# A two-layer convolution kernel: the deformable layer's hats put off by four slots, and half of the projection's loads issued by ScalarE

## The chip, the core and the metric

The kernel runs on one core of a Trainium2 chip. The core has five engines that work beside each other: TensorE (PE in the profile), VectorE (DVE), ScalarE (ACT), GpSimd (POOL) and SyncE (SP, which here only issues DMAs). The time is the device time of one launch in microseconds (us). Between two versions of this kernel the median of a few runs is compared.

## The reference

The input `x` is 32 images of 96 channels and 56 x 56 pixels in float32. Two layers follow each other.

```python
def layer0(x):                                   # inverted bottleneck, 96 -> 576 -> 96 channels
    h = silu(bn(conv1x1(x, fake_quant(w1))))
    h = silu(bn(depthwise3x3(h, fake_quant(w2))))
    s = silu(mean_over_pixels(h) @ se_w1.T + se_b1)
    s = sigmoid(s @ se_w2.T + se_b2)
    return x + bn(conv1x1(h * s, fake_quant(w3)))

def layer1(x):
    mag = abs(rfft2(x))                          # ca: channel weights from mag
    y = x * ca * sa                              # sa: a map from mean, norm and spectrum of x
    aux = concat([y, coord, resize(mean(abs(rfft2(y))))])
    offset = conv3x3(aux, off_w) + off_b         # 9 taps x (x, y)
    gate = sigmoid(conv1x1(relu(conv3x3(aux, dg1_w))))
    y_base = conv3x3(aux, base_w) + base_b
    sampled = bilinear(y, grid + offset)         # 9 samples for every pixel
    y_def = einsum("bcthw,oct->bohw", sampled, def_w) + def_b
    z = (1 - gate) * y_base + gate * y_def
    return relu(batchnorm_over_the_batch(z) + x)
```

## The kernel before

**The pipeline.** `layers` (L943) is one software pipeline over the images. Its main loop runs over 224 bands, seven to an image, each with eight rows of pixels. For a band it samples the deformable layer's inputs in two halves, and beside that it runs two streams for images ahead: `first`, which is `hidden` (L204: layer 0's expansion and depthwise convolution for the image two ahead), and `second`, which is `attend` (L438: squeeze, projection, residual and spectral attention for the image one ahead).

A band has 17 *slots*: seven in each half, and three at its end. In each slot the generator for the band two ahead, `find(n + 2)`, which is `offsets` (L645), takes one step, in the first 14 of them. Then `pump()` raises the slot's number, lets each stream take the steps that are due by then, and runs the closures in the list `later` whose slot has come:

```python
            later.sort(key=lambda e: e[0])
            while later and later[0][0] <= slot:
                later.pop(0)[1]()
```

The instructions are given out in this order. SyncE keeps it strictly. On the other engines a scheduler may reorder them, except for those wrapped in `keep_in_program_order`.

**The hats.** `offsets` computes a band's offsets (`at`, by TensorE and VectorE), writes them to DRAM (`od`, issued by GpSimd, L659), and reads them back repeated over 112 partitions: `ht`, issued by SyncE at L671 some six slots before its use. The *hats* are the bilinear weights max(0, 1 - |position - block row|): an Abs (L674, kept in program order) and a Relu (L675), both on ScalarE and in place. `hd` is their copy in DRAM, issued by ScalarE (L678). `weights_load` (L682) later reads `hd` back twice, as `wc` (L689) and `wr` (L690), four DMAs on SyncE for a half band; `weights` (L694) multiplies the two on VectorE (L696). `sample_tiles` (L717) then takes the samples with matmuls (L725) against `wc`, ScalarE copies them out to `v` (L729), `pack` (L733) moves some of them to the upper partitions (L736, ScalarE), and `deform` (L739) accumulates the result in PSUM (`pd`) with the matmuls of L744.

In the order given out, a band's Abs and Relu come just before the last `pump()` of its second half, and so stand before and between that half's packs.

**The projection.** `hidden` leaves its result in DRAM (`h2d`) as nine units of 128 partitions: four channel chunks of the image's upper half, one with the last 64 channels of both halves, four of the lower half. `attend` projects it in four quarters, each with seven rows of the upper and seven of the lower half. For each, `project_loads` (L302) loads the rows in two halves, each with a tile and a buffer of its own: half 0 has the upper half's four units (784 KB, `hq0`), half 1 the other five (980 KB, `hq1`). The pools `hq` and `ht` have one buffer for each name, so a load waits until the last reader of the load before is done. `project` (L316) runs half 0's matmuls (L324), then half 1's (L324 and L330). `attend` gives out half 0's load of the next quarter one step after half 0's matmuls of this one:

```python
            outs = project(nc, p, rows)
            next(outs)
            yield
            if q + 1 < NQ:
                first = project_loads(nc, p, h2d, q + 1, 0)
```

The first quarter's half 0 is loaded before `squeeze` (L280), whose small activations on ScalarE (L288, L294) compute the scale `s` for layer 0's last weights.

**Other lines in the text.** L153 and L169/L173 are layer 0's expansion (matmul, then activation into `hp`), L262 the depthwise taps on VectorE, L371/L394/L414 parts of the spectral transform, L606/L626 the joint convolution and its activation into `hid`, L629 and L640 copies of the base convolution, L711/L713 the transposes of the image blocks, L783 the combination of a finished band. After the bands comes `normalise` (L1298) without matmuls.

Of the kernel before, what the change touches and what calls it, by code (L numbers as in the profile page):

```python
# [7 lines left out]
FP = mybir.dt.float32  # L8
I32 = mybir.dt.int32
AF = mybir.ActivationFunctionType  # L10
# [23 lines left out]
EW = ER * W  # L34
NBD = H // RB
BW = NBW
TS = 4
NTX = W // TS
# [4 lines left out]
SB = TS + 2 * REACH  # L43
NS = SB * SB
KP = NTAP * TP
# [256 lines left out]
def project_loads(nc, p, h2d, q, half):  # L302

    u0, u1 = ((0, NCH - 1), (NCH - 1, len(UNITS)))[half]
    hq = p["hq"].tile([128, u1 - u0, EW], FP, name=f"hq{half}")
    nc.sync.dma_start(hq, h2d[u0:u1, :, q * EW : (q + 1) * EW].rearrange("u p n -> p u n"))
    return [(UNITS[u][0], hq[:, u - u0]) for u in range(u0, u1)]


# [128 lines left out]
def attend(tc, p, b, x, h2d, pooled, x1, given=False):  # L438
# [7 lines left out]
    if not given:  # L446
        NQ = HH // ER
        first = project_loads(nc, p, h2d, 0, 0)
        yield from squeeze(nc, p, pooled)
        rows = [first, project_loads(nc, p, h2d, 0, 1)]  # L450
        for _ in range(2):
            yield
        for q in range(NQ):
            at = q, q + NQ
            xrs = [residual_load(nc, p, x, k) for k in at]
# [6 lines that stand above are left out]
            os = next(outs)  # L462
            if q + 1 < NQ:
                rows = [first, project_loads(nc, p, h2d, q + 1, 1)]
            yield
            for k, o, xr in zip(at, os, xrs):
                nc.gpsimd.tensor_tensor(o, o, xr, ALU.add)  # L467
                nc.gpsimd.dma_start(x1[:, k * EW : (k + 1) * EW], o)
            yield
# [150 lines left out]
def joint_conv(nc, p, yp, j, hid):  # L620


    w = p["w"]
    pa = bank(p)
    conv3(nc, pa[:, :BW], w["joint"], yp, CJ, j)
    nc.scalar.activation(hid, pa[:DMID, :BW], AF.Relu, bias=w["dg1b"][:DMID])  # L626
    yb = p["yb"].tile([C, BW], FP, name="yb")
    yield yb, pa[OFF0 : OFF0 + NOFF, :BW]
    nc.scalar.activation(yb[BC:], pa[OFF0 + QC :, :BW], AF.Identity, bias=w["cv"]("base_b")[BC:])  # L629
    pb = bank(p)  # L630
    for k in range(NTAP):
        dy, dx = divmod(k, 3)
        r0 = j * RB + dy + PD - 1
        for i in range(2):
            nc.tensor.matmul(pb[i * BC : (i + 1) * BC, : BW // 2].rearrange("p (h w) -> p h w", h=RB // 2), w["base"][:, k],  # L635
                             yp[:C, r0 + i * RB // 2 : r0 + (i + 1) * RB // 2, dx + PD - 1 : dx + PD - 1 + W],
                             start=(k == 0), stop=(k == NTAP - 1))
    yield
    for i in range(2):
        nc.scalar.activation(yb[:BC, i * BW // 2 : (i + 1) * BW // 2], pb[i * BC : (i + 1) * BC, : BW // 2], AF.Identity,  # L640
                             bias=w["cv"]("base_b")[:BC])
    yield


def offsets(nc, p, yp, j, top, hid, ybs, hds):  # L645

    w = p["w"]
    joint = joint_conv(nc, p, yp, j, hid)  # L650
    yb, pa = next(joint)
    ybs.append(yb)
    at = p["off"].tile([NOFF, NTX, 2, TP], FP, name="at")
    for s in range(2):
        nc.vector.tensor_copy(at[:, :, s].rearrange("o t (r c) -> o t r c", r=TS),  # L655
                              pa[:, s * BW // 2 : (s + 1) * BW // 2].rearrange("o (r t c) -> o t r c", r=TS, t=NTX))
    yield
    od = p["dp"].tile([NTX, 2, NOFF, TP], FP, name="od")
    nc.gpsimd.dma_start(od.rearrange("t s o p -> o (t s) p"), at.rearrange("o t s p -> o (t s) p"))  # L659
    yield  # L660
    next(joint)
    yield
    next(joint)
    yield
    next(joint, None)
    nc.vector.tensor_reduce(top, at.rearrange("o t s p -> o (t s p)"), AX.X, ALU.max, apply_absolute_value=True)
    for _ in range(4):
        yield
    ht = p["ht"].tile([SB * NTX, 4, KP], FP, name="ht")
    src = od.rearrange("t s o p -> t (s o p)").unsqueeze(0).to_broadcast([SB, NTX, 4 * KP])  # L670
    nc.sync.dma_start(ht.rearrange("q n k -> q (n k)"), src)  # L671
    for _ in range(6):
        yield
    p["tc"].keep_in_program_order(nc.scalar.activation(ht, ht, AF.Abs, bias=w["blk"]))  # L674
    nc.scalar.activation(ht, ht, AF.Relu, bias=w["one"], scale=-1.0)  # L675
    yield
    hd = p["dp"].tile([4, SB, NTX, KP], FP, name="hd")
    nc.scalar.dma_start(hd.rearrange("x i t n -> (i t) x n"), ht)  # L678
    hds.append(hd)


def weights_load(nc, p, hd, h):  # L682
# [237 lines left out]
def padded(nc, p, a, images):  # L920

    cp = p["cp"]
    yps = [cp.tile([CJ, HY, WY], FP, name=f"yp{i}") for i in range(images)]
    for t in yps:
        nc.gpsimd.memset(t, 0.0)
        nc.sync.dma_start(t[C : C + 4, PD : PD + H, PD : PD + W], a["coord"])
        nc.sync.dma_start(t[CA:, PD : PD + H, PD : PD + W], a["place"])
    p["x2"], p["n_x2"] = [cp.tile([2 * H, CG, WX], FP, name=f"x2_{i}") for i in range(3)], 0
    for t in p["x2"]:
        nc.gpsimd.memset(t, 0.0)  # L930
    p["s4"] = [cp.tile([H, 3, WP], FP, name=f"s4_{i}") for i in range(2)]
    for t in p["s4"]:
        nc.gpsimd.memset(t, 0.0)
    return yps
# [8 lines left out]
def layers(tc, a, dp, x1d, zd, stats, far):  # L943
# [6 lines left out]
    nc = tc.nc  # L950
    B = x1d.shape[0]
    with ExitStack() as ctx:
        p = {"tc": tc, "dp": ctx.enter_context(tc.tile_pool(name="l1d", bufs=3, space=DRAM))}
# [3 lines left out]
        yp, = padded(nc, p, a, 1)  # L957
        top = p["cp"].tile([NOFF, NBD + 1], FP, name="top")
# [20 lines left out]
        streams, later = [], []  # L979
        slot = 0  # L980
# [96 lines left out]
        bands = [(b, j) for b in range(B) for j in range(NBD)]  # L1077
        hids, gates, ybs, hds, ready = [], [], [], [], []

        def find(n):  # L1080
            if n % 2 == 0:
                hids.append(p["hid"].tile([2 * NS, BW], FP, name="hid"))
            hid = hids[n // 2][n % 2 * NS : n % 2 * NS + DMID]
            return offsets(nc, p, yp, bands[n][1], top[:, n % NBD : n % NBD + 1], hid, ybs, hds)

        for n in range(2):
            for _ in beside(find(n)):
                pass
# [20 lines left out]
        for n, (b, j) in enumerate(bands):  # L1109
            if j == 0:  # L1110
                st = p["st"].tile([C, NBD, 6], FP, name="st")
            if j == turn:
                drain()
                refill(b + 1, 3 * RB)
                flush()
                start(b + 1, slots)
            more = find(n + 2) if n + 2 < len(bands) else iter(())
            next(more, None)
            for h in range(2):
# [385 lines left out]
```

## Time and profile before

| | us |
|---|---|
| runs | 9247.16, 9256.04, 9267.85 |
| median | 9256.04 |
| profiled execution, its time | 9239.07 |
| its span in the trace | 9237.3 |
| TensorE, VectorE, ScalarE, GpSimd busy | 8221.8, 7198.1, 5369.4, 2529.9 |
| TensorE waits for `hq` (L324), 31 times | 155.8 |
| TensorE waits for the packs (L744), 73 times | 201.6 |
| ScalarE waits for `ht` (L674), 98 times | 270.2 |

The mean granted clock of TensorE in the profiled execution is 0.933 of full speed. An image takes some 273 us in the middle of the run.

How the lines of the profile are read: a line of a timeline has the start, the length, the engine, the source line, the operation, its output and input, and the number of instructions that were put together; in square brackets stand the idle time of the engine before it and what ended that. In the list of waits each line has the engine and the instruction that waited, what released it, and the total, the number and the longest of such waits. SPq and ACTq are the sequencers of SyncE and ScalarE, as they issue DMAs. Line numbers are those of the kernel before.

### The profile page before, as it was taken

The numbers are of one execution on the slowest core, as the hardware profiler recorded it, in microseconds if no ns is written. First come the engines' busy times: TensorE is split into PE (matmuls) and PEld (weight loads), VectorE is DVE, ScalarE is ACT, GpSimd is POOL, SyncE is SP. The second block draws the span as 40 slices with busy tenths as digits, with TensorE's granted clock in tenths as the row PEclk, the third lists the DMA queues.
The fourth block names the chain that finished last, engine by engine and source line by source line (L and its number), as shares of the span: only waits on it lengthen the run. The fifth ranks groups of instructions, "written<-read, shape, count | busy, mean of one in ns | idle before, by whom it ended". The sixth has DMA issues, their size and how long they took to land. (4 is left out here: it accounts for less than half of the span.)

```text
span 9237.3 us, 138081 instructions
## 1 busy us (share of the span) xinstructions
PE 8221.8 (89%) x52406; PEld 5208.4 (56%) x52406; DVE 7198.1 (78%) x6693; ACT 5369.4 (58%) x10486; POOL 2529.9 (27%) x2611
## 2 busy tenths in 40 slices
PE   5889999999999999899999999999999999999870
PEld 3455565565555556555555655555565655655550
DVE  7587788888888888887888888788888888887333
ACT  2355566666666566665566665566666655666553
POOL 0123233323223322332332223233222323322210
PEclk9889999999999999999999999999999999999985
DMA  2345555555555555555555555555555555554559
GB/s 88 95 137 156 165 166 159 165 150 150 161 163 163 163 164 149 150 157 165 163 157 160 148 153 157 164 167 159 159 152 153 160 166 163 160 160 140 131 181 417
DMA packets 1068764, 1486.54 MB, mean 161 GB/s; under 512 B 590190, under 2 KB 839838, under 8 KB 1055806
## 3 DMA queue, kind: packets, MB, share of 16 engines
q1 hardware_dynamic: 858995, 985.20, 39.2%
q10 hardware_dynamic: 153803, 329.80, 9.8%
q0 software_dynamic: 55296, 162.60, 6.8%
q8 instruction: 421, 6.90, 0.3%
q14 instruction: 249, 2.04, 0.1%
HBM read 1064.29 MB, written 412.65 MB: 160 GB/s over the span
## 5 line engine op out<-in xcount | busy, mean ns | idle before, releaser
L262 DVE SCALAR_TENSOR_TENSOR acch<-hp,w,acch 128x1512 f32<-128x1512 f32 (+1 forms) x2250 | 4397.3, 1954 | 38.2
L606 PE MATMUL mm<-yp,c_jointW 104*128 104x448 f32 x4032 | 1674.2, 567 | 27.7 <-ACT sq L414 19.2
L744 PE MATMUL pd<-v,c_def 128*96 128x224 f32 (+1 forms) x6272 | 1450.9, 378 | 225.2 <-ACT v L736 201.6
L707 POOL COPY ybl<-yp 96x448 f32<-96x448 f32 x896 | 1079.8, 1232 | 1698.5 <-PE mm L711 1697.5
L744 PEld LDWEIGHTS pd<-v,c_def 128*96 128x96 f32 (+1 forms) x6272 | 1046.2, 174 | 524.7 <-ACT v L736 229.2
L606 PEld LDWEIGHTS mm<-yp,c_jointW 104*128 104x128 f32 x4032 | 772.4, 196 | 808.1 <-issue 737.9
L725 PE MATMUL mm<-wc,yt 64*96 64x144 f32 x12544 | 1065.7, 298 | 56.8 <-ACT hp L173 38.0
L169 PE MATMUL mm<-xt,w 96*128 96x392 f32 (+3 forms) x2688 | 1061.2, 529 | 36.4 <-DMA xt<-in_x 33.0
L173 ACT ACTIVATE hp<-mm,sh,inv 128x392 f32<-128x392 f32 (+2 forms) x1216 | 813.2, 673 | 445.4 <-PE mm L169 400.6
L696 DVE TENSOR_TENSOR wc<-wc,wr 128x1008 f32<-128x1008 f32 x448 | 579.5, 1293 | 622.2 <-DMA wr<-hd 614.4
L729 ACT COPY v<-mm 96x288 f32<-96x288 f32 (+1 forms) x2688 | 1001.7, 443 | 100.3 <-PE mm L725 61.3
L725 PEld LDWEIGHTS mm<-wc,yt 64*96 64x96 f32 x12544 | 830.6, 162 | 358.5 <-issue 171.3
L324 PE MATMUL mm<-hq,w3s 128*96 128x392 f32 x2048 | 798.4, 537 | 157.2 <-DMA hq<-h2d 155.8
L635 PE MATMUL mm<-yp,c_base0W 96*64 96x224 f32 x8064 | 828.0, 357 | 0.0
L736 ACT COPY v<-v 32x448 f32<-32x448 f32 x1344 | 755.2, 562 | 29.9
L659 POOL DMA_DIRECT2D od<-at x224 | 186.0, 830 | 1947.6 <-DVE at L655 1386.0
L635 PEld LDWEIGHTS mm<-yp,c_base0W 96*64 96x64 f32 x8064 | 553.2, 135 | 276.2 <-issue 69.3
L713 ACT COPY yt<-mm 128x384 f32<-128x384 f32 (+1 forms) x896 | 350.1, 440 | 519.2 <-PE mm L711 514.5
L324 PEld LDWEIGHTS mm<-hq,w3s 128*96 128x96 f32 x2048 | 340.7, 175 | 513.6 <-issue 323.7
L222 ACT ACTIVATE acch<-acch,sh,inv 128x1568 f32<-128x1568 f32 x288 | 488.6, 1696 | 207.3 <-DVE acch L262 205.0
L626 ACT ACTIVATE hid<-mm,c_dg1b 50x448 f32<-50x448 f32 x224 | 140.7, 628 | 794.7 <-PE mm L606 784.6
L467 POOL TENSOR_TENSOR o<-o,xc 96x392 f32<-96x392 f32 x256 | 366.3, 1431 | 679.3 <-ACT o L334 677.8
(194 smaller groups left out, 9038.8 us busy)
## 6 DMA issues: line engine op xcount, KB each, us to landing
h2d<-acch ACTq DMA_DIRECT2D x288, 784.0 KB
wc<-hd SPq DMA_DIRECT2D x896, 252.0 KB
wr<-hd SPq DMA_DIRECT2D x896, 252.0 KB
hq<-h2d SPq DMA_DIRECT2D x128, 980.0 KB
hq<-h2d SPq DMA_DIRECT2D x128, 784.0 KB
x<-x1d SPq DMA_DIRECT2D x768, 98.0 KB
ht<-od SPq DMA_DIRECT2D x224, 252.0 KB
hd<-ht ACTq DMA_DIRECT2D x224, 252.0 KB
```

What stands on the lines that cost most here:

```text
L169: nc.tensor.matmul(pt[p0 : p0 + w1.shape[1], : rows * W], w1, xts[hf][:, r0 * W : (r0 + rows) * W], start=True, stop=True)
L173: nc.scalar.activation(h1[lo:hi, row0 : row0 + rows, 1 : 1 + W], pt[lo:hi, : rows * W].rearrange("p (h w) -> p h w", h=rows), AF.Silu, bia ...
L262: nc.vector.scalar_tensor_tensor(acc[:, lo:hi], win, wk, acc[:, lo:hi], ALU.mult, ALU.add)
L324: nc.tensor.matmul(pts[half][:C, :EW], w3s[:, ch], hq, start=(i == 0), stop=False)
L606: nc.tensor.matmul(view, weights[:, k], yp[:channels, r0 : r0 + RB, dx + PD - 1 : dx + PD - 1 + W], start=(k == 0), stop=(k == NTAP - 1))
L635: nc.tensor.matmul(pb[i * BC : (i + 1) * BC, : BW // 2].rearrange("p (h w) -> p h w", h=RB // 2), w["base"][:, k], yp[:C, r0 + i * RB // 2 ...
L696: p["tc"].keep_in_program_order(nc.vector.tensor_tensor(wc, wc, wr, ALU.mult))
L707: nc.gpsimd.tensor_copy(yb[:, :, s], blocks)
L725: nc.tensor.matmul(pt[k][:C, (t - lo) * KP : (t - lo + 1) * KP], yt[ps, t], s[ps, t * KP : (t + 1) * KP], start=True, stop=True)
L729: nc.scalar.copy(v[:C, :, lo:hi, k].rearrange("c k t p -> c t k p"), pt[k][:C, : (hi - lo) * KP].rearrange("c (t k p) -> c t k p", t=hi - ...
L736: nc.scalar.copy(v[C:, 1 + 2 * i : 3 + 2 * i], v[i * QC : (i + 1) * QC, KA:])
L744: nc.tensor.matmul(out.rearrange("c q (t x) -> c t q x", x=TS), p["w"]["def"][ks, k], v[ks, k].rearrange("c t s (r x) -> c t (s r) x", r=T ...
```

## The change

The three last steps of `offsets` (Abs, Relu, the write of `hd`) become a function that is put into `later`, four slots further on. The step in which it is put there lies before the band's 14th `pump()`, so it runs in the band's 17th. `hds.append(hd)`, from which the weight loads take `hd`, moves with it. And half 0's loads are issued by ScalarE in program order, while half 1's stay with SyncE.

```diff
@@ project_loads
     hq = p["hq"].tile([128, u1 - u0, EW], FP, name=f"hq{half}")
-    nc.sync.dma_start(hq, h2d[u0:u1, :, q * EW : (q + 1) * EW].rearrange("u p n -> p u n"))
+    src = h2d[u0:u1, :, q * EW : (q + 1) * EW].rearrange("u p n -> p u n")
+    if half:
+        nc.sync.dma_start(hq, src)
+    else:
+        p["tc"].keep_in_program_order(nc.scalar.dma_start(hq, src))
     return [(UNITS[u][0], hq[:, u - u0]) for u in range(u0, u1)]
@@ offsets
-def offsets(nc, p, yp, j, top, hid, ybs, hds):
+def offsets(nc, p, yp, j, top, hid, ybs, hds, defer):
...
     for _ in range(6):
         yield
-    p["tc"].keep_in_program_order(nc.scalar.activation(ht, ht, AF.Abs, bias=w["blk"]))
-    nc.scalar.activation(ht, ht, AF.Relu, bias=w["one"], scale=-1.0)
-    yield
-    hd = p["dp"].tile([4, SB, NTX, KP], FP, name="hd")
-    nc.scalar.dma_start(hd.rearrange("x i t n -> (i t) x n"), ht)
-    hds.append(hd)
+
+    def hats():
+        p["tc"].keep_in_program_order(nc.scalar.activation(ht, ht, AF.Abs, bias=w["blk"]))
+        nc.scalar.activation(ht, ht, AF.Relu, bias=w["one"], scale=-1.0)
+        hd = p["dp"].tile([4, SB, NTX, KP], FP, name="hd")
+        nc.scalar.dma_start(hd.rearrange("x i t n -> (i t) x n"), ht)
+        hds.append(hd)
+
+    defer(hats)
@@ layers, find
-            return offsets(nc, p, yp, bands[n][1], top[:, n % NBD : n % NBD + 1], hid, ybs, hds)
+            return offsets(nc, p, yp, bands[n][1], top[:, n % NBD : n % NBD + 1], hid, ybs, hds,
+                           lambda hats: later.append((slot + 4, hats)))
```

## The prediction

> **What bounds the kernel now.** I read the page's busy line first, then the waits, then the timeline of one image (number 13, 3990 to 4268 us), then a table of windows over it.
>
> ```profile
> PE 8221.8 (89%) x52406; PEld 5208.4 (56%) x52406; DVE 7198.1 (78%) x6693; ACT 5369.4 (58%) x10486; POOL 2529.9 (27%) x2611
> ```
>
> TensorE is the busiest, but 89% holds matmuls at half clock, and VectorE is not far behind. Which of them binds must be read by stage. The waits:
>
> ```profile
> ACT hid L626 <- PE mm L606: 784.6, 173, 13.7
> DVE wc L696 <- DMA wr<-hd: 614.4, 133, 19.1
> ACT ht L674 <- DMA ht<-od: 270.2, 98, 7.4
> PE pd L744 <- ACT v L736: 201.6, 73, 8.0
> PE mm L324 <- DMA hq<-h2d: 155.8, 31, 9.9
> ```
>
> TensorE's own large waits are the last two, and the change touches both: L324 is the projection's first half waiting for its rows (31 times, once in each image but one), L744 the deformable matmul waiting for ScalarE's packs. The third says why the packs may be late: ScalarE stands at the hats' Abs until `ht` has landed.
>
> **Stall A**, SyncE's queue and then TensorE:
>
> ```profile
> 3977.93 0.60 SPq L689 DMA_DIRECT2D wc<-hd  x1
> ...
> 3980.59 0.66 SPq L671 DMA_DIRECT2D ht<-od  x1
> 3983.55 9.08 SPq L306 DMA_DIRECT2D hq<-h2d  x2
> ```
> ```profile
> 3992.13 0.93 PE L169 MATMUL mm<-xt,w 96*128 96x392 f32 x2
> 3997.49 2.25 PE L324 MATMUL mm<-hq,w3s 128*96 128x392 f32 x3 [4.44 <-DMA hq<-h2d]
> ```
>
> The last quarter's first-half load is issued at 3983.55, when its buffer comes free, behind four weight loads and `ht` in the same queue. It lands about 13.9 us later, and TensorE idles 4.44 us.
>
> **Stall B**, ScalarE and then TensorE:
>
> ```profile
> 4034.25 0.55 ACT L394 COPY s<-mm 128x464 f32<-128x464 f32 x1
> 4039.20 0.78 ACT L674 ACTIVATE ht<-ht,c_blk 112x576 f32<-112x576 f32 x1 [4.40 <-DMA ht<-od]
> ...
> 4040.35 0.76 ACT L675 ACTIVATE ht<-ht,one 112x576 f32<-112x576 f32 x1
> ...
> 4041.14 0.33 ACTq L678 DMA_DIRECT2D hd<-ht  x1
> ...
> 4042.13 1.15 ACT L736 COPY v<-v 32x448 f32<-32x448 f32 x2
> ```
> ```profile
> 4042.74 3.30 PE L744 MATMUL pd<-v,c_def 128*96 128x224 f32 x8 [5.04 <-ACT v L736]
> ```
>
> ScalarE waits 4.40 us for `ht`; the packs stand behind the hats, and TensorE behind the packs. Of the 73 such waits some 31 are large like this one.
>
> The windows (columns: length, busy PE, PEld, DVE, ACT, POOL, granted clock, DMA share, GB/s) show what surrounds them:
>
> ```profile
> 3990.00:4004.00 14.00, 9.56 (x22) 4.07 (x21) 8.40 (x5) 4.55 (x8) 5.29 (x7) 0.76 0.85 264
> ...
> 4038.00:4080.00 42.00, 37.10 (x291) 24.66 (x292) 36.55 (x37) 28.51 (x54) 7.60 (x6) 0.92 0.54 147
> 4080.00:4168.00 88.00, 85.04 (x606) 54.32 (x605) 86.70 (x80) 59.26 (x122) 30.08 (x25) 1.00 0.48 129
> ```
>
> After each stall the granted clock falls to one half for about 6.8 us (3996.5 to 4003.3 after A: 0.65 us a matmul for 0.33), and the window's mean is 0.76 and 0.92. In the long stretch from 4080 VectorE is busy 86.70 of 88 us: there it binds, and TensorE's gains are paid out only as far as VectorE comes early to it.
>
> **The change, part by part.** *Hats.* Nothing is added: 224 times an Abs (0.78), a Relu (0.76) and an issue (0.33) move from before the 14th of a band's 17 slots to the 17th. In the built order they leave the place between the second half's packs and stand just before the next band's L626. ScalarE idles there already (784.6/173 = 4.5 us a wait), so 1.9 us of hats are hidden; where a band has no such wait they cost at most those 1.9 us on an engine that is 58% busy. `ht`'s wait goes too, since the load has 9 us more. `hd` is written up to 9 us later; its readers, the weight loads on SyncE's queue, come 7 to 25 us after it now, and the multiply L696 far behind, so I take 0 there. If that cover is gone, a wait like L696's 614.4/133 = 4.6 us appears. On TensorE stall B returns 5.0 idle + about 2.5 of half clock = 7.5 us an image. What is late next is VectorE.
>
> *The load.* 128 issues (0.37 us each) leave SyncE for ScalarE, where each waits for the buffer and holds what follows; the second half's loads stay. On SyncE the half-0 loads no longer hold weight loads and x loads behind them, which I put at 0 (below nothing is possible). By quarter:
> - Last quarter: the issue can't come before 3983.55, but no longer queues behind the weights. Alone, the 784 KB take 3 us of packets; beside the weight loads I take 9.4 us in all, landing at 3993 where TensorE wants them at 3993.06. ScalarE stands 1.5 us at the issue. Of 4.4 to 5.0 us of stall (155.8/31) and 2.9 of half clock, I leave 0.7 for a late landing and return 6.6 to 7.2.
> - Second and third: free at the same time or 2.4 us later, with matmuls further away: 0.
> - First quarter: this load used to be issued some 20 us early (3918.8). ScalarE, in its order, reaches it after L288 at about 3939:
>
> ```profile
> 3938.83 0.25 ACT L288 ACTIVATE s<-acc,seb 24x1 f32<-24x1 f32 x1
> ```
> ```profile
> 3946.48 2.87 PE L324 MATMUL mm<-hq,w3s 128*96 128x392 f32 x8
> ```
>
> The margin is 7.6 to 8.4 us in every image, with four weight loads and `ht` on the other queue until 1.2 us after the need. A new wait of 0 to 4 us; I take 2.5, near the middle, since the packet records show another ScalarE transfer (`h2d`) stretched from 1.8 us alone to 7.3 us beside weights, and `hd` packets alternating one for one with them.
>
> A rule speaks against this part. The Trainium skill, "DMA: Bandwidth & Descriptors", section "Issuing engines are not separate DMA queues", says that transfers from all issuing engines end up on the same 16 DMA engines and that issuing from several saves only sequencer time; by it A would stay, and the sum would be B's part on VectorE alone, 2.3 × 31 = 71 us. The rows above say that A's load is behind others in one queue while packets of two queues alternate, so I go by the rows.
>
> *Sum.* TensorE: idle 155.8 + 201.6, half clock 31 × (2.9 + 2.5) = 167: 524 us in all; less 31 × (2.5 + 0.7) = 99, 425 us. VectorE must follow. Between 3990 and 4076 it idles 20 us, of which 2.93 and 4.68 wait for weight loads (stay), and 3.24, 0.43, 2.51 and 2.32 for things that TensorE's lateness delays: 8.5 us can go, 11.3 with the ping-pong against L414. So the gain is 8.5 − 2.5 (the new first-quarter wait) = 6.0 us an image, × 31 = 186 us. The profiled execution took 9239.07 us (span 9237.3), 17 us under the median of the three runs: 9239 − 186 + 17 = 9070. With 11.3 and a new wait of 0 it is 350 us (8906), with 8.5 − 4 it is 140 (9116).
>
> **Rivals.**
> - *VectorE does not cap.* It has 78%, and the order around 4080 may shift so that all of TensorE's 425 us are paid: 8831. Against it: 86.70 of 88.
> - *Mostly eaten.* The first-quarter wait lets the clock drop (2.5 to 4 + 2.9), so that 8.5 is nearly gone: 8.5 − 6.9 = 1.6 × 31 = 50, or with 8.5 − 5.4 = 3.1, 96: 9160 to 9206; with more of the same, 9225, and if the load only trades A for that wait, no change.
> - *Slower: ScalarE's load crawls.* If 3 us become 12 beside the weight loads, as `h2d` stretched fourfold, and about 2 us pass before the first packet, the first quarter waits 14 − 8 = 6.1 us and 2.9 of half clock, 9.0 in all; the last quarter's load lands at 3997.7, so A stays, and only B's part on VectorE (2.3) is gained: 6.7 × 31 = 208 slower, 9464. It decides from about a threefold stretch: the first quarter then loses 3.1 + 2.9 us and A keeps 1.6 of its idle and the clock, which leaves nothing of the 8.5. For it: `h2d`. Against: that transfer's packets are 6 KB and beside 4 KB ones, and the weight loads end shortly after the need.
> - *It doesn't do what it says.* Excluded for the hats by the built order; for the load only the landing time can tell.
>
> **How the numbers follow.** Main case 0.52 (8906 to 9116), TensorE's full gain 0.16, mostly eaten 0.18 (0.06 of it within 0.2%), slower 0.14. A difference of 0.2%, 19 us, is about what this measurement tells from no change. Faster 0.52 + 0.16 + 0.12 = 0.80, same 0.06, slower 0.14. The range runs from the full gain (8832) to the eaten case's end (9225), leaving out the slower case and the very edge.
>
> **What would show it.** B right: L744 ← L736 falls from 201.6 to under 60, and L674 no longer waits for `ht`. A right: L324's wait for `hq` moves from the last to the first quarter and is about half. VectorE's cap right: its busy share rises from 78% to 80% and it stays above 95% after 4080. Wrong if L324's wait grows above 155.8, if the clock's mean doesn't rise over 0.933, or if L696 ← `wr` grows by more than 100 us, which would mean that `hd` or the weight loads became the late ones.

## The result and the profile after

The changed kernel is slower: 9326.14 us against 9251.6 us (medians of four runs each), a ratio of 1.0083 with a 95% interval of 1.0062 to 1.0104, some 75 us; the time lies above the predicted range, which ended at 9225. Its profiled execution took 9348.17 us, the longest of its four, with a span of 9346.4 us. Lines below the first diff have moved: L324 is now L328, L674 L680, L696 L703, L736 L743, L744 L751, and L306 has become L308 (SyncE, half 1) and L310 (ScalarE, half 0).

The page's busy line and the waits that answer to those of before:

```profile
PE 8363.4 (89%) x52406; PEld 5260.0 (56%) x52406; DVE 7172.3 (77%) x6693; ACT 5379.0 (58%) x10486; POOL 2592.9 (28%) x2611
```
```profile
DVE wc L703 <- DMA wr<-hd: 712.8, 133, 18.4
ACT hid L630 <- PE mm L610: 660.3, 161, 12.6
...
PE mm L328 <- DMA hq<-h2d: 201.0, 64, 8.8
...
PEld mm L391 <- DVE sq L377: 91.9, 31, 6.3
...
PE pd L751 <- ACT v L736: 16.1, 35, 0.9
```

Stall B is off the list: the deformable matmul's wait for the packs, 201.6 us before, is gone, and the 16.1 us that remain wait for a copy. But TensorE's wait for the projection's rows has grown from 155.8 us in 31 waits to 201.0 in 64: two in an image in place of one. And a wait that was not on the list before has come, the spectral matmul L391 for VectorE's reductions, 31 times.

The new wait for `hq`, in the first quarter of image 14: ScalarE's issue, then TensorE.

```profile
4258.63 0.38 ACTq L310 DMA_DIRECT2D hq<-h2d  x1
```
```profile
4266.59 1.22 PE L732 MATMUL mm<-wc,yt 64*96 64x144 f32 x16
4272.13 1.57 PE L328 MATMUL mm<-hq,w3s 128*96 128x392 f32 x2 [4.32 <-DMA hq<-h2d]
```

13.5 us from the issue to the first matmul. The last quarter's load on the same queue, behind SyncE's weight loads and `ht`:

```profile
4305.23 0.59 SPq L696 DMA_DIRECT2D wc<-hd  x1
...
4307.84 0.66 SPq L675 DMA_DIRECT2D ht<-od  x1
```
```profile
4310.11 0.37 ACTq L310 DMA_DIRECT2D hq<-h2d  x1
```
```profile
4319.34 0.93 PE L169 MATMUL mm<-xt,w 96*128 96x392 f32 x2
4325.74 1.59 PE L328 MATMUL mm<-hq,w3s 128*96 128x392 f32 x2 [5.48 <-DMA hq<-h2d]
```

No weight load stands in front of it in its queue any more, and yet 15.6 us pass before its first matmul. Where stall B was, VectorE now stands at the weights' multiply, and TensorE behind VectorE:

```profile
4367.29 1.21 DVE L703 TENSOR_TENSOR wc<-wc,wr 128x1008 f32<-128x1008 f32 x1 [7.63 <-DMA wr<-hd]
...
4369.36 1.15 DVE L377 TENSOR_REDUCE sq<-mm 112x56 f32<-112x448 f32 x2
```
```profile
4370.03 1.15 PE L391 MATMUL mm<-c_FU,x 112*128 112x116 f32 x8 [2.90 <-DVE sq L377]
```

L391 needs a PSUM bank that L377's reductions set free, and these stand in VectorE's order behind the multiply. Over 28 images, 15 of these waits end with L377 as here, and 12 with the landing of `x`, the transform's own input, which SyncE loads. The windows over image 14 (columns as before: length, busy PE, PEld, DVE, ACT, POOL, granted clock, DMA share, GB/s) show the first quarter, the last quarter, the place of stall B, and the long stretch:

```profile
4266.00:4282.00 16.00, 11.69 (x50) 5.99 (x49) 12.09 (x8) 5.94 (x13) 1.33 (x3) 0.89 0.33 107
4318.00:4332.00 14.00, 8.52 (x18) 3.58 (x17) 6.98 (x5) 2.31 (x4) 4.21 (x6) 0.76 0.80 268
4366.00:4408.00 42.00, 37.94 (x288) 23.44 (x287) 38.31 (x38) 27.16 (x53) 9.29 (x6) 0.92 0.58 148
4408.00:4496.00 88.00, 86.14 (x601) 54.93 (x602) 83.85 (x78) 55.59 (x114) 26.96 (x23) 0.96 0.47 129
```

Both places keep a clock of 0.76 and 0.92, and the first quarter, at full clock before, has 0.89.

**One image, stage by stage.** TensorE gives out its work in almost the same order in all these kernels, so the time between two of its own instructions can be compared. The table gives mean us over 28 images, worked out from the traces between starts of L324/L328 and L744/L751; in brackets TensorE's idle time and the time at half clock. "Last" runs from the third quarter's second half to the last quarter's second half and holds stall A; "next" is the band and a half after it; "B" holds stall B.

```
                 first          quarters 2-3  last           next           B              rest           image
before            7.9 (0.0,0.0)  38.2         23.0 (5.0,6.6) 22.2 (0.0,0.0) 41.3 (6.2,7.9) 136.9          269.5
changed          14.9 (3.6,5.0)  38.8         19.8 (2.7,2.9) 22.3 (0.1,0.0) 40.3 (3.6,6.9) 136.0          272.1
hats_only         8.0 (0.0,0.1)  38.2         23.0 (4.9,6.5) 22.2 (0.0,0.0) 40.2 (3.6,6.7) 136.9          268.4
loads_only       13.7 (3.1,3.9)  38.8         19.9 (2.7,3.2) 22.3 (0.1,0.0) 41.2 (6.2,7.8) 136.4          272.3
first_on_sync     8.0 (0.0,0.0)  38.8         20.4 (2.6,4.8) 22.3 (0.0,0.0) 40.2 (3.8,6.3) 136.7          266.4
hats_mul3         9.8 (0.0,1.8)  38.2         23.2 (5.2,6.7) 28.7 (3.0,7.1) 38.5 (3.7,3.1) 137.6          275.9
wide_packets     10.5 (1.1,0.7)  38.8         16.1 (0.3,0.1) 25.7 (1.9,3.3) 39.9 (3.5,6.7) 135.9          266.8
hats_wide         8.0 (0.0,0.1)  38.2         22.8 (4.9,6.5) 22.2 (0.0,0.0) 40.4 (3.8,6.7) 136.5          268.1
first_sync_mul1   8.1 (0.0,0.3)  38.8         19.7 (2.5,3.2) 22.5 (0.2,0.2) 40.5 (3.8,7.0) 140.6          270.3
first_sync_again  8.0 (0.0,0.1)  38.8         20.2 (2.6,4.1) 22.2 (0.0,0.0) 40.3 (3.5,7.1) 136.3          265.8
sync_wide_again   8.0 (0.0,0.1)  38.8         16.2 (0.4,0.1) 26.2 (2.0,4.0) 39.5 (3.5,5.7) 136.4          265.0
```

In the table the changed kernel loses 6.9 us an image at the first quarter and 0.7 before the third quarter's second half. It gains 3.2 in "last", 1.0 at stall B and 0.9 in the rest. The sum, 2.6 us more an image, times 31 is 80 us, close to the 75 us of the medians.

A part of these differences is work that changed its place. Counted by instruction, two of the third quarter's matmuls (L334, 0.65 us) stand in "quarters 2-3" and not in "last" wherever ScalarE issues the loads of quarters two to four. Where it issues the first quarter's too, the ten small matmuls of L291 (1.2 us) stand in "first" and not in the rest, in every second image. Without this moved work the first quarter loses 6.3 us an image, the stretch before the third quarter's second half loses nothing, stall A gives back 2.6, and the rest 0.3.

### The profile page after: what moved, and what is told of

Read it like the earlier page. It is cut to its first block, busy times and chain, and to the rows that moved or that the text cites. A ratio compares the mean times of both kernels' runs of the same rounds, so it can differ in the third digit from the quotient of the medians.

```text
span 9346.4 us, 137984 instructions
## 1 busy us (share of the span) xinstructions
PE 8363.4 (89%) x52406; PEld 5260.0 (56%) x52406; DVE 7172.3 (77%) x6693; ACT 5379.0 (58%) x10486; POOL 2592.9 (28%) x2611
## 5 line engine op out<-in xcount | busy, mean ns | idle before, releaser
L610 PE MATMUL mm<-yp,c_jointW 104*128 104x448 f32 x4032 | 1714.0, 578 | 4.2 <-ACT yt L720 1.9
L714 POOL COPY ybl<-yp 96x448 f32<-96x448 f32 x896 | 1107.5, 1263 | 1802.8 <-PE mm L718 1802.4
L751 PE MATMUL pd<-v,c_def 128*96 128x224 f32 (+1 forms) x6272 | 1417.5, 373 | 19.6 <-ACT v L736 16.1
L610 PEld LDWEIGHTS mm<-yp,c_jointW 104*128 104x128 f32 x4032 | 792.1, 200 | 804.5 <-issue 766.8
L751 PEld LDWEIGHTS pd<-v,c_def 128*96 128x96 f32 (+1 forms) x6272 | 1036.9, 172 | 305.6 <-issue 79.8
L732 PE MATMUL mm<-wc,yt 64*96 64x144 f32 x12544 | 1108.9, 301 | 106.1 <-ACT hp L173 47.4
L703 DVE TENSOR_TENSOR wc<-wc,wr 128x1008 f32<-128x1008 f32 x448 | 577.1, 1288 | 775.3 <-DMA wr<-hd 712.8
L169 PE MATMUL mm<-xt,w 96*128 96x392 f32 (+3 forms) x2688 | 1072.5, 538 | 38.4 <-DMA xt<-in_x 33.4
L732 PEld LDWEIGHTS mm<-wc,yt 64*96 64x96 f32 x12544 | 856.7, 163 | 434.4 <-issue 191.3
L736 ACT COPY v<-mm 96x288 f32<-96x288 f32 (+1 forms) x2688 | 1006.9, 442 | 114.1 <-PE mm L732 76.7
L328 PE MATMUL mm<-hq,w3s 128*96 128x392 f32 x2048 | 834.6, 557 | 208.1 <-DMA hq<-h2d 201.0
L743 ACT COPY v<-v 32x448 f32<-32x448 f32 x1344 | 755.2, 562 | 29.8
L328 PEld LDWEIGHTS mm<-hq,w3s 128*96 128x96 f32 x2048 | 352.5, 181 | 596.8 <-issue 526.2
L471 POOL TENSOR_TENSOR o<-o,xc 96x392 f32<-96x392 f32 x256 | 387.5, 1514 | 856.7 <-ACT o L338 849.5
L720 ACT COPY yt<-mm 128x384 f32<-128x384 f32 (+1 forms) x896 | 350.1, 440 | 444.0 <-PE mm L718 443.1
```

Of the source, the lines that this page charges most:

```text
L169: nc.tensor.matmul(pt[p0 : p0 + w1.shape[1], : rows * W], w1, xts[hf][:, r0 * W : (r0 + rows) * W], start=True, stop=True)
L328: nc.tensor.matmul(pts[half][:C, :EW], w3s[:, ch], hq, start=(i == 0), stop=False)
L610: nc.tensor.matmul(view, weights[:, k], yp[:channels, r0 : r0 + RB, dx + PD - 1 : dx + PD - 1 + W], start=(k == 0), stop=(k == NTAP - 1))
L703: p["tc"].keep_in_program_order(nc.vector.tensor_tensor(wc, wc, wr, ALU.mult))
L714: nc.gpsimd.tensor_copy(yb[:, :, s], blocks)
L732: nc.tensor.matmul(pt[k][:C, (t - lo) * KP : (t - lo + 1) * KP], yt[ps, t], s[ps, t * KP : (t + 1) * KP], start=True, stop=True)
```

## The experiments

### The two halves of the change by themselves

Hats put off, all loads by SyncE (`project_loads` as in the kernel before):

```diff
-    if half:
-        nc.sync.dma_start(hq, src)
-    else:
-        p["tc"].keep_in_program_order(nc.scalar.dma_start(hq, src))
+    nc.sync.dma_start(hq, src)
```

> Only the hats are put off; all projection loads stay on SyncE. Theory (the load is what costs, the hats are worth little): of the changed kernel's stages only the one around the old stall B gains, 1.0 to 2.0 us an image, so 31 to 62 us faster than before (ratio 0.993 to 0.997); L744 <- packs under 30 us, L324 <- hq about 156 as before, no wait at the first quarter. Rival (the late hd is what costs: the weights come later to VectorE): as slow as the changed kernel or slower, ratio 1.005 or more, and VectorE's wait for wr at 700 us or more.

And the loads alone, with `offsets` as before:

```diff
-    nc.sync.dma_start(hq, src)
+    if half:
+        nc.sync.dma_start(hq, src)
+    else:
+        p["tc"].keep_in_program_order(nc.scalar.dma_start(hq, src))
```

> Only half 0's loads go to ScalarE; the hats stay where they were. Theory: the first quarter loses 6.9 us an image, the last quarter gains 3.2, the third loses 0.65, so +4.3 us x 31 = 134 us slower than before (ratio about 1.0145); L744 <- packs stays near 200. Rival (the hats are the slow part): faster than before by 100 us.

Measured: hats alone 9202.45 us against 9256.67 before, ratio 0.9939 (0.9927 to 0.9951), 54 us faster; loads alone 9341.93 us, ratio 1.0104 (1.009 to 1.0117), 85 us slower. The waits of the hats alone, then of the loads alone:

```profile
DVE wc L699 <- DMA wr<-hd: 506.8, 127, 18.2
...
PE mm L324 <- DMA hq<-h2d: 152.1, 31, 7.6
...
PEld mm L387 <- DVE sq L373: 87.9, 31, 4.6
...
PE pd L747 <- ACT v L732: 17.5, 35, 1.2
```
```profile
PE pd L748 <- ACT v L740: 205.8, 75, 8.9
...
PE mm L328 <- DMA hq<-h2d: 178.9, 62, 7.2
```

So the load is what costs, and the hats are a gain. With the hats alone VectorE's wait for `wr` falls (614.4 to 506.8): the later `hd` delays no weights, and the 712.8 of the changed kernel came with the loads, which alone bring it to 741.7. What the loads alone cost was less than expected (85, not 134 us): by the table they lose 5.8 us an image at the first quarter, not 6.9. The two parts do not add up to the whole, 85 − 54 = 31 against 75: in the table 1.1 us of that difference an image is the first quarter's. There the load's last packet comes 12.3 us after its issue with the hats put off and 11.8 without, and more weight packets pass beside it (218 for 161); why is not shown.

### The first quarter's load back on SyncE

```diff
-    if half:
+    if half or q == 0:
         nc.sync.dma_start(hq, src)
```

> Hats put off, the loads of quarters two to four on ScalarE, the first quarter's back on SyncE. Theory: the first quarter's 6.9 us an image go and the rest stays: 2.6 - 6.9 = -4.3 us x 31 = 134 us faster than before (ratio 0.9855). Rival (ScalarE's queue does nothing for the last quarter; its stall was only shorter because TensorE came to it later): like the hats alone, 31 to 62 us faster, L324 <- hq back at about 156.

9155.96 us, ratio 0.989 (0.9878 to 0.9903): 101 us faster than before and 170 us faster than the change. The first quarter is back at 8.0 us, without any wait:

```profile
DVE wc L703 <- DMA wr<-hd: 445.1, 123, 17.2
...
PE mm L328 <- DMA hq<-h2d: 84.3, 32, 8.0
```

One load in four, issued on ScalarE 0.6 to 0.7 us ahead of L288 in every image, where SyncE had issued it some 20 us earlier, makes the difference between 0.8% slower and 1.1% faster. The rival here is refuted: the other three loads on ScalarE's queue do shorten stall A (155.8 to 84.3 us), but leave 2.6 us of idle and most of the half clock.

### Why ScalarE's loads are late: the width of the packets

The trace's packet records of the changed kernel show one and the same transfer, 784 KB in 512 packets of 1568 bytes on ScalarE's queue, under two conditions (means over 28 images, us from the issue):

```
                 first packet   last packet
quarter 2            1.1            3.9        little beside it
quarter 1            1.4           12.3        four weight loads (256 packets of 4032 bytes) and ht
quarter 4            2.9           12.1        the same, and the half-1 load ahead
```

While the weights run, some 47 of its packets pass in a microsecond (512 in 10.9 us), beside some 20 to 35 of theirs; alone 183 pass (512 in 2.8 us). If the engines take turns packet by packet, wider packets must help it. So `h2d` was laid out by quarters: the same bytes and queues, but a load of half 0 has 128 packets of 6272 bytes (and the writes have 1568 in place of 6272).

```diff
-        nc.scalar.dma_start(h2d[u], flat)
+        nc.scalar.dma_start(h2d[:, :, u].rearrange("q p n -> p q n"), flat.rearrange("p (q n) -> p q n", n=EW))
...
-    src = h2d[u0:u1, :, q * EW : (q + 1) * EW].rearrange("u p n -> p u n")
+    src = h2d[q, :, u0:u1]
...
-            h2d = p["dp"].tile([len(UNITS), 128, HB], FP, name="h2d")
+            h2d = p["dp"].tile([HH // ER, 128, len(UNITS), EW], FP, name="h2d")
```

> The changed kernel with h2d laid out by quarters, so that a projection load's packets are 6272 bytes (half 0) and 7840 bytes (half 1) in place of 1568, four and five times fewer of them; its writes become 1568 bytes. Bytes and queues stay. Theory (ScalarE's queue and SyncE's take turns packet by packet, so a load of 512 small packets beside weight packets of 4032 bytes gets a small share): the last packet of the first quarter's load comes 6 to 8 us after its issue in place of 12.3, of the last quarter's 7 to 9 in place of 12.1; both waits of L324's successor go, and the kernel is 5 to 9 us an image, 155 to 280 us, faster than the changed kernel (9050 to 9170 us, ratio to before 0.978 to 0.991). Rival (the 16 engines share out bytes, whatever the packets): last packets still over 11 us after the issue, and the time of the changed kernel, 9326 within 30 us.

9158.39 us, ratio 0.99 (0.9883 to 0.9917), 168 us faster than the change, with only the layout of `h2d` altered (half 1's packets and the writes with it). The last packet of the first quarter's load comes at 9.1 us in place of 12.3, of the last quarter's at 9.2 in place of 12.1; quarter 2, which has no company, hardly moves (3.9 to 3.7). The rival, a share of the bytes whatever the packets, is out. In the first quarter, while only weight packets run beside it, the narrow load passes 48 packets a microsecond beside 26 of theirs, 0.41 of the bytes; the wide one passes 17 beside 24, 0.53 of the bytes, and both together move more (204 GB/s for 181). So width raises a load's share, but the turns are not one for one, and the theory's 6 to 8 and 7 to 9 us were both too short. TensorE's idle at the first quarter falls from 3.6 to 1.1 us, at stall A from 2.7 to 0.3:

```profile
PE mm L328 <- DMA hq<-h2d: 45.6, 37, 3.3
```

A control on whether wide packets are simply faster: the same layout with all loads on SyncE, where weights and loads share one queue.

> Hats put off, all loads on SyncE, h2d laid out by quarters (wide packets). A control on what wide packets do by themselves. Theory (they help only where two queues take turns): in SyncE's one queue the last quarter's load still stands behind the weight loads, its stall stays within 1 us of the 4.9 us idle of the hats alone, and the time is that of the hats alone, 9202 within 30 us. Rival (wide packets are simply faster): the stall is gone or under 2 us, as with ScalarE's queue and wide packets, and the time is near 9131.

9214.32 us, ratio 0.9968 (0.9957 to 0.9979), within 30 us of the hats alone (0.3% above them by the ratios, whose intervals do not meet). Stall A stays whole, 4.9 us idle an image:

```profile
PE mm L324 <- DMA hq<-h2d: 150.5, 31, 7.8
```

So to take stall A away needs both, a queue of its own and wide packets.

### What holds the place of stall B

With the hats out of the way, TensorE's idle at B fell only from 6.2 to 3.6 us. The trace says that VectorE stands at the multiply; so the multiply was given out three slots later:

```diff
-                        ready.extend(weights(nc, p, *ws) for ws in loads[:1])
+                        for ws in loads[:1]:
+                            later.append((slot + 3, lambda ws=ws: ready.append(weights(nc, p, *ws))))
```

> Hats put off, all loads on SyncE, and VectorE's multiply of the weights (wc <- wc, wr) given out three slots later. Theory (what took stall B's place is VectorE standing at that multiply until wr lands, with the reductions behind it that free TensorE's PSUM banks): VectorE's wait for wr falls from about 700 us to under 400, the spectral matmul's wait for VectorE's sq goes, and the kernel gains 3 to 6 us an image beyond the hats alone, 120 to 240 us faster than before (ratio 0.974 to 0.987). Rival (the buffers of wr come free later and SyncE's weight loads with them): no faster than the hats alone, with a new wait of TensorE for wc at the sampling matmuls.

9473.03 us, ratio 1.024 (1.0223 to 1.0257): much slower. Half of the theory is borne out: VectorE's wait falls (506.8 us with the hats alone, 212.9 here), the spectral matmul's wait for `sq` is gone from the upper lines (1.9 us in all), and B shrinks by 1.7 us more, to 38.5. But TensorE's idle at B does not shrink (3.7 us, now mostly at matmuls that wait for ScalarE's L414); what fell is the time at half clock.

```profile
PE mm L728 <- issue: 224.8, 79, 10.2
...
DVE wc L699 <- DMA wr<-hd: 212.9, 74, 17.0
```

The rival was right about the time: TensorE now waits at the sampling matmuls L728 (224.8 us, which the profile puts down to nothing that it shows). The trace tells for what: in 77 of these waits, 223.9 us in all, the matmul starts 0.1 us after VectorE's multiply ends. But in 76 of the 77 the multiply had not waited for `wr`; it came straight behind other work of VectorE. So it is not a late landing of the weights, as the rival had it, that makes these waits, but a multiply that stands too late in VectorE's order. One slot, on the kernel with the first load on SyncE, was tried too:

> As the kernel with the first quarter's load back on SyncE, and VectorE's multiply of the weights given out one slot later (three slots made the hats-only kernel 270 us slower). Theory (the weights land late for TensorE too, so the wait only changes its engine): no faster, 0 to 70 us slower than that kernel, 9156 to 9226 us, the sampling matmuls waiting more. Rival (one slot is free for TensorE and takes VectorE's standing away from the reductions): 1 to 1.5 us an image, 30 to 45 us faster, 9110 to 9125 us.

9268.52 us, ratio 1.0025 (1.0013 to 1.0037), 113 us slower than without it, beyond both expectations. Here L391's wait for `sq` stays as it was (87.6 us), and the loss lies in the rest, 3.9 us an image. There L169 now waits for ScalarE's copy into `yt` (L720), 73.6 us in all where it was 3.5; why is not shown. The two runs say that moving this multiply is not free, and that with it moved L391's wait goes while the idle time at B stays. What bounds this place is left open.

### A version that beats both

Hats put off, the first quarter's load on SyncE, and wide packets:

> As the kernel with the first quarter's load back on SyncE, but with h2d laid out by quarters. Theory (packet turns): only the last quarter's stall is left to win, 2.6 us idle and about 2 us of half clock, of which VectorE lets 2 to 4 us an image through: 60 to 125 us faster than that kernel, 9030 to 9095 us (ratio to before 0.976 to 0.983). Rival (bytes): 9156 within 30 us, the wait for hq still 2.6 us an image.

9131.46 us, ratio 0.9882 (0.9863 to 0.9901). The interval meets that of the narrow packets, so the two were run again side by side:

> The kernel with the first quarter's load back on SyncE again, beside the next one on the same chip: 0.989 of before, within 0.002.

> The same with wide packets again, beside the run above. Theory: the 1.1 us an image that its trace showed less than the one above, x 31 = 35 us, are real: 20 to 50 us faster than that one. Rival: no difference beyond 15 us, since what the last quarter gains is given back at the pd bank two bands later.

Narrow 9136.76 us, ratio 0.9878 (0.9863 to 0.9893); wide 9118.96 us, ratio 0.9862 (0.9847 to 0.9877). Wide is ahead by 18 us in the medians, 0.7 us × 31 = 22 in the traces, between the theory's 20 and the rival's 15, and the intervals meet; that it is faster than before by some 129 us, 1.4%, is clear. The expected 2 to 4 us an image did not come, and the table says where they went. Stall A is gone with all its half clock: "last" takes 16.2 us, 6.9 less than before, of which 0.65 is the moved work and 6.2 to 6.3 the stall. "Next" takes 3.9 more than before, with 2.0 us of idle time that was not there, mostly for VectorE's combination of a band (L790, 1.65 us). The row among the waits, and one such wait in image 14:

```profile
PE pd L751 <- DVE z L790: 48.3, 23, 3.2
```
```profile
4251.29 1.06 PE L751 MATMUL pd<-v,c_def 96*96 96x224 f32 x2 [2.58 <-DVE z L790]
```

TensorE is early at the single `pd` bank, VectorE has not yet combined the band before, and 4.0 us at half clock follow.

## Why the prediction was wrong, point by point

- **The step that failed** is the landing time of a load on ScalarE's queue beside the weight loads. I took 9.4 us for the last quarter and a wait of 2.5 us for the first. Both loads have their last packet 12 us after the issue, and the first matmul comes after 12.9 and 13.1. So the first quarter waits 3.6 us, and as this lies inside the bound of 0 to 4, what undid this term was also the other half of that stall: 5.0 us at half clock, which I had priced only in the rivals. Idle time and the half of 5.0 us make 6.1 of the 6.3 us an image lost there, where the sum had 2.5. The issue itself came where I had put it. Term by term, in us an image: the sum had 6.2 from A, 2.3 from B and -2.5 at the first quarter; the runs show 2.6, 1.0 and -6.3, and 0.3 in the rest.
- **Stall A** was to return 6.6 to 7.2 us; it returned 2.6, since of 5.0 us of idle 2.7 stayed. That ScalarE's queue frees it from standing behind the weights was right, and with wide packets it returned 6.2 to 6.3, near what I had asked of it. What I missed is that a queue of one's own buys only a share of the DMA engines: with 1568-byte packets beside 4032 that was 0.41 of the bytes.
- **The slower rival** had the mechanism: a fourfold stretch, 14 us to land, a first-quarter wait of 6.1 with 2.9 of half clock. I gave it 0.14 because `h2d` has wide packets and this load narrow ones. That argument ran the wrong way: the narrow load got 0.41 of the bytes beside weights and the wide one 0.53. Its price, 208 us, was too high, as A gave back 2.6 us where the rival had nothing, and the first quarter lost 6.3, not 9.0.
- **Stall B**: the hats' move did on ScalarE what was said. L744's wait for the packs fell from 201.6 us to 0.8 (I had said under 60; the 16.1 us that L751 still waits are for the copies of L736, 22.8 before), and ScalarE's wait for `ht` from 270.2 to 16.2. "What is late next is VectorE" was right too; but I let 2.3 us an image through, and the place gained 1.0 to 1.1. What took the stall's place is open in part. VectorE waits there for the weights, a row that I had read (4.68 us) and put down as staying, without asking which of TensorE's matmuls stands behind it.
- **VectorE's cap**: the 8.5 us that could go were never asked for in full by the changed kernel. With wide packets A's part was: TensorE won 6.2 to 6.3 us at A, and 3.9 came back in "next", as 2.0 us of idle time, mostly for VectorE at `pd`, and 4.0 at half clock. So VectorE does cap the gain, but here it shows through one PSUM bank in the band and a half after A, and not in the full stretch after 4080.
- **The late `hd`** cost nothing, as I had taken. The sign that I named for the opposite, L696's wait up by more than 100 us, all but appeared (98 us), and came from the loads. The other two signs of being wrong did appear: L324's wait for `hq` grew above 155.8 us, and the mean clock, at 0.929, did not rise over 0.933.
- The rule that I weighed against the change, from the Trainium skill's "DMA: Bandwidth & Descriptors", section "Issuing engines are not separate DMA queues" (all issuers' transfers share the same engines; only sequencer time is saved), left 71 us for the hats alone and nothing for A. Hats alone measured 54. For A the rule says too little here, since the other queue took 2.3 us off its idle; but on the load as a whole it was the better guide than my reading of one-for-one turns. That reading was wrong in the kernel before, too: with only weight packets beside them, 49 `hd` packets pass in a microsecond for 35 of theirs.

## What to carry to other kernels

A load that is moved to another engine's queue is also moved to another place in time: it is issued when that engine's order reaches it, and a margin that an idle issuer gave away freely (here 27 us before the first matmul, then 13, of which TensorE stood waiting 3.6) must be asked for first, load by load. A queue of its own lets a transfer overtake what stood ahead of it, but beside other traffic it gets a share that grows with its packets (here 0.41 of the bytes, then 0.53), so price it from a contended transfer with packets of its size or narrower, and try wider packets. Add the half clock after a new stall to the stall's price in the main case and not only in the rivals.

## What the runs showed of the hardware

The same transfer, 784 KB in 512 packets of 1568 bytes, took 3.9 us from issue to last packet without company and 12.3 us beside weight loads on the other queue. Laid out as 128 packets of 6272 bytes, it took 3.7 and 9.1 us: the width hardly matters alone and decides beside others, and in one queue with the weights (the control) it took nothing off the stall, 4.9 us idle either way. And a stall of 3 to 4 us on TensorE cost almost twice its length: at the first quarter 3.6 us of idle time brought 5.0 us at half clock and 6.3 us in all.
